# Two probability triangles merged into one square before the transposes, and parted by masks behind them

## The chip, the cores and the metric

The kernel runs on one core of one Trainium2 chip. The metric is the device time of one execution, in microseconds; the comparison uses the median of several runs. A NeuronCore has five engines, each with its own queue of instructions that is worked off in order: TensorE (PE, matrix multiplications and transposes, which write PSUM; PEld is its weight load), VectorE (DVE), ScalarE (ACT), GpSimd (POOL) and SyncE (SP, which issues most DMAs). POOL works on SBUF alone here, and it also issues the gathers.

## The reference

One layer over 4096 tokens of 256 numbers, all in fp32. It adds two branches to the input: a windowed attention block with its feed-forward part, and a mixture of experts (8 experts, the best 2 for each token, 816 hidden units). Both read the normalized input. The change lies in the attention, with 8 heads of 32 numbers:

```python
band = jnp.abs(qi[:, None] - (kj[None, :] - w)) <= w          # w = 64
scores = jnp.einsum('bhcqd,bhckd->bhcqk', q, k3) * scale
scores = jnp.where(allow, scores, jnp.float32(-1e+30))
p = jax.nn.softmax(scores, axis=-1)
o = jnp.einsum('bhcqk,bhckd->bhcqd', p, v3)
...
attn = o @ Wo + bo
x = _layernorm(x + attn, gamma, beta)
h = jax.nn.gelu(x @ W1 + b1, approximate=False)
x = x + (h @ W2 + b2)
```

So a query at position t looks at the keys from t - 64 to t + 64: 129 keys.

## The kernel before

The kernel has four stretches. First come the normalization, the router's logits, the first keys, queries and values, and the table that sorts tokens by expert (to about 82 us). Then a loop of 34 steps, in which each step computes one unit of expert work, a pair of token tiles (256 tokens) or a single one (128). The first 32 steps (`STEPS`) also carry attention. After the loop come five units that may turn out empty (`whole`, from 852 to 888 us), and last the attention branch's feed-forward part with the final sum.

An attention step works on a pair of query tiles i and i + 1 (j is 0 or 1) of 128 queries, and on one half hq of the heads, four heads hh. Even steps have hq = 0, odd steps hq = 1. The queries of a tile look at 256 keys, which start 64 before the tile, so the row of query r has its 129 allowed keys at columns r to r + 128 of these 256. In other words, the first 128 columns hold an upper triangle with its diagonal, the last 128 columns a lower triangle with its diagonal; the rest is zero after the exponential, because the mask has put -1e30 there.

The functions of a step, in the order in which the loop calls them:

- `gather` (L783) issues, on POOL, the indirect DMAs that fetch the tokens of a unit two steps ahead into `xs`, which has three buffers.
- `scores` (L893): 16 half-height matmuls on PE (`ps`, L901) into four PSUM banks; then DVE adds the mask, writes `pr` and keeps the negated maximum (`nm`, L915). `pr` is [128 queries, 4 heads, 2 tiles, 256 keys] and has one buffer.
- `exps` (L927): eight exponentials of 128x256 on ACT (L930), each with its sum; they are called in three portions, with the first two chunks of the expert's up and gate products (`chunk`, L814 on PE, L822 on ACT, L823 on DVE) between them.
- `closing` (L992), in even steps: the output projection of the pair before (L996), the residual's sum and the moments on DVE. `residual` (L985) follows: SP loads a tile and POOL adds the bias (L989).
- `scale` (L939): the reciprocal of the sums, and eight products of 128x256 on DVE (L944), one for each head and tile.
- `down` (L866): the down projection of the unit before (L858, 28 matmuls), its bias on DVE (L871), the store; then the load of the next `wd` on SP.
- `turned` (L796): the transposes of the next unit's tokens (L801) and the copy to `xsT` on DVE (L806). In the steps 1 to 16 a projection for later keys, queries or values follows.
- chunk 2, `flip` for j = 0, chunk 3, `flip` for j = 1. `flip` (L948) transposes, for each half k of the 256 keys, four heads into one PSUM bank (L953), and copies the bank to SBUF as `prT`, on ACT for k = 0 (L960), on DVE for k = 1 (L958).
- chunks 4 and 5, the rest of the hidden units (`glu_rest`, L831), the silu's on ACT (L853).
- `weigh` (L964): 32 matmuls, with 32 columns of `vts` as weights and `prT` as the moving side (L968), into the bank `po`.
- `outputs` (L976), in odd steps only: four activations on ACT (L980) that add `bv` and write `oT`, two for each tile.

The order is written out by hand (`manual_schedule`): each engine runs its instructions in the order of the program's text. All PSUM tiles but `po` share seven banks in rotation (`bank`): a tile gets the bank of the tile seven before it, once that one's reader is through.

Of the kernel before, what the change touches and what calls it, by code (L numbers as in the profile page):

```python
# [41 lines left out]
P = 128  # L42
# [57 lines left out]
def block_kernel(ctx: ExitStack, tc: tile.TileContext, a: dict, out: bass.AP):  # L100
# [23 lines left out]
    def bank(name):  # L124
        return psm.tile([P, G], F32, tag="bank", name=name)

    def halves(pb):
        return pb.rearrange("p (t n) -> p t n", t=2)
# [32 lines left out]
    def bcast(ap, n, at):  # L161

        shape = list(ap.shape)
        shape.insert(at, n)
        return ap.unsqueeze(at).to_broadcast(shape)
# [51 lines left out]
    att = ctx.enter_context(ExitStack())  # L217
    wqkv = pool(att, "wqkv", right)
    mask = wqkv.tile([P, 4, 2 * P], F32, tag="mask", name="mask")
    bqs = wqkv.tile([P, DC], F32, tag="bqs", name="bqs")  # L220
    xnT = wqkv.tile([P, DC, S + 2 * WIN], F32, tag="xnT", name="xnT")
    nc.gpsimd.memset(xnT[:, :, 0:WIN], 0.0)
# [80 lines left out]
    def make_mask():  # L303

        nc.gpsimd.memset(mask, 0.0)
        for kind in range(4):

            def keep(base, step, channel, m=mask[:, kind, :]):  # L310
                nc.gpsimd.affine_select(
                    out=m,
                    in_=m,
                    compare_op=ALU.is_ge,
                    fill=MASKED,
                    base=base,
                    pattern=[[step, 2 * P]],
                    channel_multiplier=channel,
                )

            keep(0, 1, -1)
            keep(2 * WIN, -1, 1)
            if kind == 0:
                keep(-WIN, 1, 0)
            if kind == 3:
                keep(2 * P - WIN - 1, -1, 0)


    with ExitStack() as early:
# [597 lines left out]
    def exps(pr, nm, sums, lo, hi):  # L927
        for n in range(lo, hi):
            hh, j = n // 2, n % 2
            nc.scalar.activation(  # L930
                pr[:, hh, j, :],
                pr[:, hh, j, :],
                AF.Exp,
                bias=nm[:, j, hh : hh + 1],
                scale=-1.0,
                accum_out=sums[:, j, hh : hh + 1],
            )

    def scale(i, hq, pr, sums):  # L939
        rec = sp.tile([P, 2, HQ], F32, tag="rec", name=f"rec{i}_{hq}")  # L940
        nc.vector.reciprocal(rec, sums)
        for j in range(2):
            for hh in range(HQ):
                nc.vector.tensor_scalar(  # L944
                    pr[:, hh, j, :], pr[:, hh, j, :], rec[:, j, hh : hh + 1], None, ALU.mult
                )

    def flip(i, hq, j, pr):  # L948
        prT = []
        for k in range(2):  # L950
            pb = bank(f"pT{i}_{hq}_{j}{k}")
            for hh in range(HQ):
                nc.tensor.transpose(  # L953
                    pb[:, hh * P : (hh + 1) * P], pr[:, hh, j, k * P : (k + 1) * P], ident
                )
            t = sp.tile([P, G], F32, tag="prT", name=f"prT{i}_{hq}_{j}{k}", bufs=4)
            if k:
                nc.vector.tensor_copy(t, pb)  # L958
            else:
                nc.scalar.copy(t, pb)  # L960
            prT.append(t)
        return prT

    def weigh(i, hq, j, prT, po):  # L964
        for k in range(2):
            for hh in range(HQ):
                h = hq * HQ + hh
                nc.tensor.matmul(  # L968
                    po[hh * DH : (hh + 1) * DH, j, hq, :],
                    vts[i + j + k][:, h * DH : (h + 1) * DH],  # L970
                    prT[k][:, hh * P : (hh + 1) * P],
                    start=(k == 0),
                    stop=(k == 1),
                )

    def outputs(i, j, po):  # L976

        oT = sp.tile([P, DC, P], F32, tag="oT", name=f"oT{i + j}")
        for c in range(DC):
            nc.scalar.activation(  # L980
                oT[:, c, :], po[:, j, c, :], AF.Identity, bias=bv[:, c : c + 1]
            )
        return oT

    def residual(i):  # L985

# [2 lines left out]
        nc.gpsimd.tensor_tensor(res, res, bcast(bo, 2, 1), ALU.add)  # L989
        return res  # L990

    def closing(i, oTs, res):  # L992
        pw = halves(bank(f"wo{i}"))
        for j in range(2):
            for c in range(DC):
                nc.tensor.matmul(  # L996
                    pw[:, j, :], oTs[j][:, c, :], Wo[:, c, :], start=(c == 0), stop=(c == DC - 1)
                )
        nc.vector.tensor_tensor(res, pw, res, ALU.add)
        for j in range(2):  # L1000
            moments(mv2[:, i + j, :], res[:, j, :], f"b{i + j}")
        nc.sync.dma_start(out=rows(x1d, i, 2), in_=res)
# [111 lines left out]
    for b in range(ALWAYS):  # L1114

        i, hq = b // 2 * 2, b % 2
        attends = b < STEPS
        hT = hTs[b % 2][:, :, 0 : UNITS[b][1] * P]

        def chunk(f):  # L1120
            glu(b, f, gus[b], xT[b], hT)

        if b + 2 < ALWAYS:
            xs[b + 2] = gather(b + 2)
        if attends:
            pr, nm, sums = scores(i, hq)
        if b == 0:
            xT[0] = turned(0, xs.pop(0))
        if attends:
            exps(pr, nm, sums, 0, 3)  # L1130
        chunk(0)
        if attends:
            exps(pr, nm, sums, 3, 6)
        chunk(1)
        if attends:
            exps(pr, nm, sums, 6, 8)
        if hq == 0 and i - 2 in res:
            closing(i - 2, oTs.pop(i - 2), res.pop(i - 2))
            if i < STEPS:
                res[i] = residual(i)  # L1140
        if attends:
            scale(i, hq, pr, sums)
        if b == STEPS:
            att.close()
            wf = pool(ctx, "wf", right)
            hf = pool(ctx, "hf", right, bufs=2)
            accp = pool(ctx, "accp", right, bufs=4)
            got = pool(ctx, "got", right, bufs=8)
            W1, W2 = matrix(wf, "W1", F1, DC), matrix(wf, "W2", D, FC1)
            b1 = column("b1", FC1, wf)  # L1150
            gamma, beta, b2 = (row(n, D, wf) for n in ("gamma", "beta", "b2"))

            late = pool(ctx, "late", right)
            other.update({n: late for n in range(ALWAYS, BLOCKS, 3)})
            load_unit(ALWAYS)
            for n in range(ALWAYS, BLOCKS):
                xs[n] = gather(n)
        if b == STEPS + 1:
            *_, r2 = rstd_of(mv2, root_of(mv2, NT, "b"), NT, "b")
            x2s[0] = second_loads(0)  # L1160
        if b > 0:
            down(b - 1, downs.pop(b - 1), hTs[(b - 1) % 2])
        if b == ALWAYS - 1:
            load_unit(ALWAYS + 1)
        if b + 1 < ALWAYS:
            downs[b + 1] = load_down(b + 1)
        if b + 1 < ALWAYS:
            xT[b + 1] = turned(b + 1, xs.pop(b + 1))
        else:
            for n in range(ALWAYS, BLOCKS):  # L1170
                xT[n] = turned(n, xs[n])
        g = b // TG
        if attends and g + AHEAD <= NG:
            ahead = g + AHEAD
            if b % TG == 0 and g > 0:
                for c in range(DC):
                    keys(ahead, c)
            elif ahead < NG and b % TG == 1:
                values(ahead * TG + 1, 2, False)
            elif ahead < NG and b % TG == 2:  # L1180
                values(ahead * TG + 3, 2, False)
            elif ahead < NG and b % TG == 3:
                for c in range(DC):
                    queries(ahead, c, False)
        chunk(2)
        if attends:
            if hq == 0:
                pos[i] = pso.tile([P, 2, DC, P], F32, tag="po", name=f"po{i}")
            prT0 = flip(i, hq, 0, pr)
        chunk(3)  # L1190
        silu(hT, 0, 2)
        if attends:
            prT1 = flip(i, hq, 1, pr)
        chunk(4)
        n = b - (ALWAYS - len(MAYBE))
        if n >= 0:
            flags[ALWAYS + n] = nc.values_load(used[0:1, n : n + 1], min_val=0, max_val=1)
        chunk(5)
        silu(hT, 2, 4)
        glu_rest(b, gus[b], xT[b], hT)  # L1200
        silu(hT, 4, FCM)
        silu(hT, FCM, FCE, slice(REM_UP, REM_UP + REM))
        if attends:
            for j, prT in enumerate((prT0, prT1)):
                weigh(i, hq, j, prT, pos[i])
            if hq == 1:
                oTs[i] = [outputs(i, j, pos[i]) for j in range(2)]
        if b + 2 < ALWAYS:
            gus[b + 2] = load_gu(b + 2)

# [124 lines left out]
```

## Time and profile before

| what | value |
|---|---|
| median of 3 runs | 1121.75 us (1121.59 to 1122.61) |
| the profiled execution | 1123.71 us, its span 1121.9 us |
| granted clock of TensorE over the span | 0.999 |
| transposes of `pr` (L953) | 512, 66.8 us busy, 273 ns each |
| exponentials (L930) | 256, 126.7 us busy |
| scaling (L944) | 256, 70.4 us busy, 350 ns each |
| POOL's sum for the residual (L989) | 16, 20.4 us busy |
| gathers of the loop (L788) | 71, 67.7 us busy on POOL |
| length of an odd step without projections | 21.74 us |
| length of an even step without projections | 23.47 us |

The lengths are from start to start of a step's first L901 on the timeline. An engine's busy time says how long it worked, not that the end depended on it. Matmuls overlap, so the time that one costs is to be read from the starts of a row of them. A group's row gives its busy time, the mean length of one, and the idle time that its engine had just before, with what ended it.

### The profile page before, as it was taken

The numbers are of one execution on the slowest core, as the hardware profiler recorded it, in microseconds if no ns is written. First come the engines' busy times: TensorE is split into PE (matmuls) and PEld (weight loads), VectorE is DVE, ScalarE is ACT, GpSimd is POOL, SyncE is SP. The second block draws the span as 40 slices with busy tenths as digits, with TensorE's granted clock in tenths as the row PEclk, the third lists the DMA queues.
The fourth block names the chain that finished last, engine by engine and source line by source line (L and its number), as shares of the span: only waits on it lengthen the run. The fifth ranks groups of instructions, "written<-read, shape, count | busy, mean of one in ns | idle before, by whom it ended". The sixth has DMA issues, their size and how long they took to land. (4 is left out here: it accounts for less than half of the span.)

```text
span 1121.9 us, 18116 instructions
## 1 busy us (share of the span) xinstructions
PE 1108.0 (99%) x6616; PEld 890.2 (79%) x6616; DVE 530.9 (47%) x1635; ACT 533.4 (48%) x1266; POOL 237.9 (21%) x264
## 2 busy tenths in 40 slices
PE   8999999999999999999999999999999999999998
PEld 6578887888888888888888888888888756666667
DVE  6656555455456455554555555545433323333213
ACT  4526456646565556656654666466423421111110
POOL 6421101011010110110101101101203075555422
PEclk9999999999999999999999999999999999999999
DMA  9162444345344443444544544344566423333112
GB/s 288 58 235 76 142 161 160 147 149 181 109 164 171 143 166 135 179 147 154 178 149 149 180 141 175 135 167 146 192 216 234 157 72 99 94 93 94 57 57 75
DMA packets 60746, 163.36 MB, mean 146 GB/s; under 512 B 6288, under 2 KB 46608, under 8 KB 51184
## 3 DMA queue, kind: packets, MB, share of 16 engines
q1 hardware_dynamic: 54176, 144.48, 37.3%
q0 software_dynamic: 6480, 17.70, 5.2%
q8 instruction: 53, 0.87, 0.3%
q14 instruction: 37, 0.30, 0.1%
HBM read 140.28 MB, written 21.89 MB: 145 GB/s over the span
## 5 line engine op out<-in xcount | busy, mean ns | idle before, releaser
L814 PE MATMUL gu<-xsT,wg 128*128 128x256 f32 (+1 forms) x1632 | 357.8, 369 | 1.1 <-ACT xsT L806 0.7
L814 PEld LDWEIGHTS gu<-xsT,wg 128*128 128x128 f32 x1632 | 288.3, 190 | 47.4 <-issue 14.9
L822 ACT ACTIVATE gs<-gu,wg 128x256 f32<-128x256 f32 (+1 forms) x204 | 92.4, 456 | 296.1 <-PE gu L814 269.4
L823 DVE SCALAR_TENSOR_TENSOR hT<-gu,wg,gs 128x256 f32<-128x256 f32 (+1 forms) x204 | 95.1, 468 | 251.6 <-ACT gs L822 243.2
L858 PE MATMUL pe<-wd,hT 128*128 128x256 f32 x896 | 198.9, 379 | 0.0
L858 PEld LDWEIGHTS pe<-wd,hT 128*128 128x128 f32 x896 | 169.9, 190 | 22.9
L989 POOL TENSOR_TENSOR res<-res,bo 128x512 f32<-128x512 f32 x16 | 20.4, 1276 | 597.2 <-DMA res<-xnd 405.7
L930 ACT ACTIVATE pr<-pr,nm 128x256 f32<-128x256 f32 x256 | 126.7, 497 | 0.4
L1052 ACT ACTIVATE hf<-ph,b 128x512 f32<-128x512 f32 x64 | 44.0, 687 | 158.2 <-PE ph L1045 148.9
L1045 PE MATMUL ph<-x2T,W 128*128 128x512 f32 x256 | 111.3, 593 | 0.8 <-DVE x2T L1037 0.8
L1083 PE MATMUL pd<-W,hf 128*128 128x256 f32 x512 | 111.7, 379 | 0.0
L915 DVE CUSTOM_DVE_ANT_0 pr<-ps,mask 128x256 f32<-128x256 f32 x256 | 90.8, 420 | 37.6 <-PE ps L901 37.6
L1083 PEld LDWEIGHTS pd<-W,hf 128*128 128x128 f32 x512 | 96.8, 190 | 13.3 <-issue 0.5
L1045 PEld LDWEIGHTS ph<-x2T,W 128*128 128x128 f32 x256 | 48.5, 190 | 58.9 <-issue 56.9
L788 POOL DMA_INDIRECT xs<-xnd,token x71 | 67.7, 953 | 82.2 <-DVE paired_tiles L755 32.8
L853 ACT ACTIVATE hT<-hT 128x512 f32<-128x512 f32 (+3 forms) x148 | 80.4, 543 | 7.6 <-DVE hT L823 4.2
L1061 POOL DMA_INDIRECT got<-done,slot x64 | 63.3, 989 | 73.9 <-DVE acc L1074 61.0
L944 DVE TENSOR_SCALAR pr<-pr,rec 128x256 f32<-128x256 f32 x256 | 70.4, 350 | 1.1
L953 PE MATMUL pT<-ident,pr 128*128 128x128 f32 x512 | 66.8, 273 | 0.4 <-DVE pr L944 0.3
L953 PEld LDWEIGHTS pT<-ident,pr 128*128 128x128 f32 x512 | 59.7, 141 | 6.7 <-PE gu L814 0.6
L1090 DVE TENSOR_TENSOR acc<-pd,acc 128x512 f32<-128x512 f32 x16 | 11.0, 691 | 83.3 <-PE pd L1083 83.3
L930 ACT ACTIVATION_READ_ACCUMULATOR pr<-pr,nm 128x1 f32 x256 | 48.5, 189 | 0.0
(193 smaller groups left out, 1164.5 us busy)
## 6 DMA issues: line engine op xcount, KB each, us to landing
wg<-in_gate_up SPq DMA_DIRECT2D x37, 1670.5 KB
wd<-in_down SPq DMA_DIRECT2D x37, 1024.0 KB
done<-y SPq DMA_DIRECT2D x30, 256.0 KB
x<-in_x SPq DMA_DIRECT2D x8, 512.0 KB
xnd<-xn SPq DMA_DIRECT2D x8, 512.0 KB
res<-xnd SPq DMA_DIRECT2D x16, 256.0 KB
x1d<-res SPq DMA_DIRECT2D x16, 256.0 KB
x<-x1d SPq DMA_DIRECT2D x8, 512.0 KB
```

What stands on the lines that cost most here:

```text
L788: nc.gpsimd.indirect_dma_start(out=x[:, t, :], out_offset=None, in_=xnd, in_offset=bass.IndirectOffsetOnAxis(ap=token[:, i : i + 1], axis=0),)
L814: nc.tensor.matmul(pb[:, k, :], w[:, lo : lo + P], xT[:, c, :], start=(c == 0), stop=(c == DC - 1),)
L822: nc.scalar.activation(gs, pb[:, 0, :], AF.Identity, bias=w[:, gb : gb + 1])
L823: nc.vector.scalar_tensor_tensor(hT[:, f, :], pb[:, 1, :], w[:, ub : ub + 1], gs, ALU.add, ALU.mult)
L853: nc.scalar.activation(hT[on, lo:hi, :], hT[on, lo:hi, :], AF.Silu)
L858: nc.tensor.matmul(pd[:, t, :], hT[:, f, t * P : (t + 1) * P], w[:, f * D : (f + 1) * D], start=(k == 0), stop=(k == FCE - 1),)
L915: nc.vector.tensor_tensor_reduce(out=pr[:, hh, j, :], in0=ps[hh][:, j, :], in1=mask[:, kind + j, :], scale=-1.0, scalar=-LOWEST, op0=ALU.a ...
L930: nc.scalar.activation(pr[:, hh, j, :], pr[:, hh, j, :], AF.Exp, bias=nm[:, j, hh : hh + 1], scale=-1.0, accum_out=sums[:, j, hh : hh + 1],)
L944: nc.vector.tensor_scalar(pr[:, hh, j, :], pr[:, hh, j, :], rec[:, j, hh : hh + 1], None, ALU.mult)
L953: nc.tensor.transpose(pb[:, hh * P : (hh + 1) * P], pr[:, hh, j, k * P : (k + 1) * P], ident)
L1045: nc.tensor.matmul(ph, W1[:, c, f * P : (f + 1) * P], x2T[:, c, :], start=(c == 0), stop=(c == DC - 1),)
L1083: nc.tensor.matmul(pd[:, u, :], hT[:, f, (t + u) * P : (t + u + 1) * P], W2[:, f, :], start=(f == 0), stop=(f == FC1 - 1),)
```

## The change

The allowed columns of the two halves complement each other: the first half holds keys with column >= row, the second keys with column <= row. They overlap in the diagonal alone. The new kernel adds the second half onto the first, so that a full square is left, and transposes only this square. Behind the transpose two masks of 0 and 1 part it again: `first_keys` keeps keys >= query (with the diagonal), `second_keys` keys < query (without it). What this can't tell apart is the diagonal, where both halves have a value. So the second half's diagonal is kept on its own: the second half is multiplied with the identity, summed along its rows to one number for each query, head and tile (`same`), and multiplied with the difference of the two value rows that belong to it (`xd`, values of the second key tile minus those of the first). This part is transposed too (`pX`, two transposes a step), and is added at the end together with `bv`.

By engines:

- POOL: `merge`, two operations of 128x256 for each head, called between the portions of `exps`; `apart`, two differences of 128x128 a step; the product of `xd` with `same`. At the start, four operations for the two masks.
- DVE: `scale` is one product of 128x1024, one reduction of 128x1024 to 8, and one product of 8. `flip` does two masked evictions for each j, the second one into the freed half of `pr`. `outputs` runs in every step, one addition of 128x256.
- ACT: no copies in `flip`, no `outputs`; one activation a step in `flip_rest`.
- PE: eight transposes in the two calls of `flip` instead of sixteen, and two in `flip_rest`.

```diff
+    first_keys = wqkv.tile([P, P], F32, tag="first_keys", name="first_keys")
+    second_keys = wqkv.tile([P, P], F32, tag="second_keys", name="second_keys")
...
+        for m, base, step in ((first_keys, 0, 1), (second_keys, -1, -1)):
+            nc.gpsimd.memset(m, 1.0)
+            nc.gpsimd.affine_select(
+                out=m,
+                in_=m,
+                compare_op=ALU.is_ge,
+                fill=0.0,
+                base=base,
+                pattern=[[-step, P]],
+                channel_multiplier=step,
+            )
...
-    def scale(i, hq, pr, sums):
+    def merge(pr, hh):
+
+        first, second = pr[:, hh, :, 0:P], pr[:, hh, :, P:]
+        nc.gpsimd.tensor_tensor(first, first, second, ALU.add)
+        nc.gpsimd.tensor_tensor(second, second, bcast(ident, 2, 1), ALU.mult)
+
+    def apart(i, hq):
+
+        xd = sp.tile([P, 2, P], F32, tag="xd", name=f"xd{i}_{hq}", bufs=1)
+        of = slice(hq * P, (hq + 1) * P)
+        for j in range(2):
+            nc.gpsimd.tensor_tensor(
+                xd[:, j, :], vts[i + j + 1][:, of], vts[i + j][:, of], ALU.subtract
+            )
+        return xd
+
+    def scale(i, hq, pr, sums, xd):
+
         rec = sp.tile([P, 2, HQ], F32, tag="rec", name=f"rec{i}_{hq}")
+        same = sp.tile([P, 2, HQ], F32, tag="same", name=f"same{i}_{hq}")
+        by_head = "p j h -> p h j"
         nc.vector.reciprocal(rec, sums)
+        first = pr[:, :, :, 0:P]
+        nc.vector.tensor_tensor(first, first, bcast(rec.rearrange(by_head), P, 3), ALU.mult)
+        nc.vector.tensor_reduce(same.rearrange(by_head), pr[:, :, :, P:], AX.X, ALU.add)
+        nc.vector.tensor_tensor(same, same, rec, ALU.mult)
+        xh = xd.rearrange("p j (h d) -> p j h d", h=HQ)
+        nc.gpsimd.tensor_tensor(xh, xh, bcast(same, DH, 3), ALU.mult)
+
+    def flip(i, hq, j, pr):
+        pb = bank(f"pT{i}_{hq}_{j}")
+        for hh in range(HQ):
+            nc.tensor.transpose(pb[:, hh * P : (hh + 1) * P], pr[:, hh, j, 0:P], ident)
+
+        prT = [sp.tile([P, HQ, P], F32, tag="prT", name=f"prT{i}_{hq}_{j}"), pr[:, :, j, P:]]
+        for t, m in zip(prT, (first_keys, second_keys)):
+            nc.vector.tensor_tensor(
+                t, pb.rearrange("p (h q) -> p h q", h=HQ), bcast(m, HQ, 1), ALU.mult
+            )
+        return prT
+
+    def flip_rest(i, hq, xd):
+
+        pb = halves(bank(f"pX{i}_{hq}"))
         for j in range(2):
-            for hh in range(HQ):
-                nc.vector.tensor_scalar(
-                    pr[:, hh, j, :], pr[:, hh, j, :], rec[:, j, hh : hh + 1], None, ALU.mult
-                )
-
-    def flip(i, hq, j, pr):
...
+            nc.tensor.transpose(pb[:, j, 0:P], xd[:, j, :], ident)
+        added = sp.tile([P, 2, P], F32, tag="added", name=f"added{i}_{hq}", bufs=1)
+        nc.scalar.activation(added, pb[:, :, 0:P], AF.Identity, bias=bv[:, hq : hq + 1])
+        return added
...
-                    prT[k][:, hh * P : (hh + 1) * P],
+                    prT[k][:, hh, :],
...
-    def outputs(i, j, po):
...
+    def outputs(i, hq, po, oT, added):
+        nc.vector.tensor_tensor(oT[:, :, hq, :], po[:, :, hq, :], added, ALU.add)
...
         if attends:
             pr, nm, sums = scores(i, hq)
+            xd = apart(i, hq)
...
             exps(pr, nm, sums, 0, 3)
+            merge(pr, 0)
         chunk(0)
         if attends:
             exps(pr, nm, sums, 3, 6)
+            merge(pr, 1)
+            merge(pr, 2)
         chunk(1)
         if attends:
             exps(pr, nm, sums, 6, 8)
+            merge(pr, 3)
...
-            scale(i, hq, pr, sums)
+            scale(i, hq, pr, sums, xd)
...
+                oTs[i] = sp.tile([P, 2, DC, P], F32, tag="oT", name=f"oT{i}", bufs=1)
             prT0 = flip(i, hq, 0, pr)
         chunk(3)
         silu(hT, 0, 2)
         if attends:
             prT1 = flip(i, hq, 1, pr)
+            added = flip_rest(i, hq, xd)
...
-            if hq == 1:
-                oTs[i] = [outputs(i, j, pos[i]) for j in range(2)]
+            outputs(i, hq, pos[i], oTs[i], added)
```

## The prediction

> **What bounds the kernel now.** I read the page's engine table first, then the window between the routing and the loop's end, then one loop step on each engine.
>
> ```profile
> PE 1108.0 (99%) x6616; PEld 890.2 (79%) x6616; DVE 530.9 (47%) x1635; ACT 533.4 (48%) x1266; POOL 237.9 (21%) x264
> ...
> PEclk9999999999999999999999999999999999999999
> ```
>
> ```profile
> 187.00:805.00 618.00, 618.00 (x4207) 527.18 (x4206) 327.99 (x1054) 363.99 (x908) 66.21 (x66) 1.00 0.45 155
> ```
>
> The columns of the second are the window, its length, busy PE, PEld, DVE, ACT, POOL, the granted clock, the DMA share and GB/s. In the attention steps TensorE has no gap: 618.00 of 618.00 us, at full clock, with DMA at 45%. DVE is busy 53%, ACT 59%, POOL 11%. So here time is PE instructions, and a cut in them is worth its own pace, as long as nothing makes PE wait. "Busy" does not give that pace, since matmuls overlap. I take it from starts on PE's timeline, in step 21 (it starts at 557.02, the first L901; columns are start and length):
>
> ```profile
> 567.69 0.60 PE L801 MATMUL pts<-ident,xs 128*128 128x128 f32 x4
> 568.13 1.89 PE L814 MATMUL gu<-xsT,wg 128*128 128x256 f32 x8
> 569.86 1.04 PE L953 MATMUL pT<-ident,pr 128*128 128x128 f32 x8
> 570.73 1.89 PE L814 MATMUL gu<-xsT,wg 128*128 128x256 f32 x8
> ```
>
> Eight transposes take 570.73 - 569.86 = 0.87 us, or 0.109 us each.
>
> The second thing to read is how long `pr` is finished before PE wants it. The same step on ACT and DVE:
>
> ```profile
> 559.65 0.49 ACT L930 ACTIVATE pr<-pr,nm 128x256 f32<-128x256 f32 x1
> ...
> 563.31 0.50 ACT L930 ACTIVATE pr<-pr,nm 128x256 f32<-128x256 f32 x1
> ```
>
> ```profile
> 563.93 0.20 DVE L941 RECIPROCAL rec<-sums 128x8 f32<-128x8 f32 x1 [0.50 <-ACT pr L930]
> 564.17 2.19 DVE L944 TENSOR_SCALAR pr<-pr,rec 128x256 f32<-128x256 f32 x8
> ```
>
> The exponentials end 6.8 us into the step, the scaling 9.35, the first pT starts at 12.84. That gap of 3.5 us is the cover for all that the change puts between exponentials and transposes. Over all 32 steps pT starts at 12.44 (step 16), 12.84 (the odd steps from 17), 13.77 (3, 7, 11, 15), 14.57 (1, 5, 9, 13 and the even ones from 18), 14.98 (4, 8, 12) and 16.08 (2, 6, 10, 14); in step 0 at 8.55, and there PE already waits for the scaling.
>
> Prices of the pieces:
>
> ```profile
> L989 POOL TENSOR_TENSOR res<-res,bo 128x512 f32<-128x512 f32 x16 | 20.4, 1276 | 597.2 <-DMA res<-xnd 405.7
> ```
>
> ```profile
> L1025 POOL TENSOR_TENSOR x<-x,beta 128x1024 f32<-128x1024 f32 x8 | 18.8, 2348 | 110.8 <-DVE x L1024 110.8
> ...
> L1024 DVE TENSOR_TENSOR x<-x,gamma 128x1024 f32<-128x1024 f32 x8 | 9.8, 1225 | 0.3
> ```
>
> **PE, per step.** Removed: 16 pT. Added: 8 pT and 2 pX. Net 6 fewer, 0.65 us a step, 192 in 32 steps: 192 x 0.109 = 20.9 us. The weighing matmuls stay in number and shape. Two other measures: by busy time (66.8 us over 512, 0.130 each) it is 25.0. The Trainium skill (TensorE: Matmul & The Clock Gate, Part 4) gives about 275 ns for a transpose in a kernel and says that transposes don't keep the clock up; 192 x 0.275 would be 52.8 us. The row agrees with 273 ns as the length of one, but lengths overlap and the granted clock is 1.00, so I take 20.9.
>
> **The Pool chain.** Between exps and scale come eight operations of 128x256, an addition and a multiplication for each head. No row has this shape. The line through 512 (1276) and 1024 (2348) is 0.204 + 2.094 ns per element, which gives 0.74 us at 256 and 0.47 at 128. Each multiplication also waits for the addition before it; L1027, which waits so for L1026, has 0.6 us of idle over 8, 0.075 each. So 0.775 on average. Bounds: half the 512 row, 0.64, and the whole 512 row, 1.28, should two short rows cost like one long one. I take the line, because both its points have row-wise operands with a broadcast too.
> The chain starts when the second exponential is read out, at about 3.3 us (even steps lose their four L980 ahead of exps, 1.14 us on ACT, so they start at the odd steps' time), and is Pool-bound: 3.3 + 8 x 0.775 = 9.5.
> The Trainium skill (GPSIMD Engine Reference, sections 3.1 Elementwise and 4.1 Engine selection) speaks against this: elementwise work belongs on VectorE, GpSimd being about twice as slow; its 4497 ns for 2048 elements makes about 0.56 at 256, an estimate without a fixed part. By it the chain would end at 7.8, by the rows at 9.5; DVE would do the eight at 0.42 (L587, two inputs of 256) in 3.4 us. The ratio is right, but the chain is paid only where it is exposed.
>
> **DVE.** Removed per step: scaling 2.19, two copies L958 at 0.683. Added: one product of 1024 (L1024's 1.225), one reduction of 1024 (L585's 0.42 for 256 and L671's 0.69 for 512 give 1.22), one of 8 (0.19), four masked evictions (0.69 like L871, PSUM with a broadcast operand), one outputs (0.42). That is 5.8 against 3.56: 2.25 more in a step of some 22 us, 63% busy. The new wait stands at the product: behind it on DVE queue y (L871), xsT (L806), the q or v evictions and chunk 2's hT. Product 9.6 to 10.85, so pT may start at 10.9 against 12.44 at the earliest: 1.5 us in hand. Reduction and `same` end at 12.3, y at 13.0 (was 11.55), xsT 13.7, hT 14.2, the first pair of masked evictions 15.6, the second 17.4, before weigh, which comes 0.65 earlier than now, at 20.07. SP's done store and wd load behind y move 1.5 us and have a whole step. PSUM rotates over seven banks: pT1 and pX need those of gu1, wo or pe, which are free by then. In the four short steps (3, 7, 11, 15) two q evictions lie in the same queue and the second masked eviction ends at 18.6 against weigh's second half at 18.45: about 0.15 each, 0.6 us together.
>
> **ACT.** Two L960 (0.576) and on average two L980 (0.368) go, one 128x256 (0.469) comes: 1.4 us less, hidden (59% busy).
>
> **Rest of Pool.** The differences (2 x 0.47) wait for the previous pX and are done before the step starts. The product with `same` waits for DVE at 12.3, ends at 13.2, and pX comes at 15.45: 2.2 in hand. In even steps it stands behind the residual, which waits for its DMA until 11.3 to 13.0: 13.4 to 15.1 against pX at 17.2 (step 16: 14.0 against 15.0). The gathers, which now run two steps ahead, will stand behind this and start 13 to 15 us into a step; they are needed more than a step later. Pool sum: about 7.9 us a step on top of 2 to 4. The four mask operations at the start fall in Pool's idle stretch from 40.3 to 73.1: nothing.
>
> **Step 0** has no down projection, so no cover: additions wait for exps (the last is read at 7.73), the chain ends at 10.1, pT starts at 11.45 instead of 8.55. The old pT0 was itself stretched to 1.5 us by the scaling, so PE is 2.4 late against its gain.
>
> **The sum.** 1123.71 (span 1121.9 and 1.8 around it) - 20.9 + 2.4 + 0.6 = 1105.8 us. The median of the runs, 1121.75, lies 1.96 lower: 1103.8.
>
> At the loop's end PE waits 0.96 us for oT (L980 on ACT), which goes to DVE; up to 2 us may be gained or lost there, left at nothing.
>
> **Rivals.**
> 1. *The Pool chain is exposed (other side).* Place: pT0's wait for the product. It ends at 3.3 + 8p + 1.33, p being Pool's time per operation. Up to p = 0.98 no step but 0 waits; at 1.21 the waits eat the 20.9. At the upper bound (1.276 and its wait, 1.31) it ends at 15.1: eight steps lose 2.26, step 16 loses 2.66, four lose 1.33, eleven 0.53, three 0.12, step 0 about 5.9: 38 us, so +17, 1139. For it: no row of this shape, and Pool's spans are rough. Against: two rows on one line. A smaller exposure, p near 1.1, costs 10 and gives 1111.
> 2. *DVE and Pool hold each other up*, or DVE's queue makes PE wait for a bank or for prT. Against: the product is the one long DVE operation with two SBUF inputs, and Pool idles then. For: 2.25 us more stand in one stretch. One microsecond exposed in each of the 31 steps that have cover gives 1135, half of that 1119.
> 3. *The transposes don't cost what they seem*, because weight loads set the pace and shift to the neighbours: then about 1121. Against: the starts show 0.87 us with nothing else running.
>
> **How the numbers follow.** Forecast 0.66; exposed chain 0.24 (0.19 slower, 0.03 faster, 0.02 no change); DVE 0.07 (0.03, 0.03, 0.01); nothing gained 0.03 (0.02 no change, 0.01 slower). So faster 0.72, same 0.05, slower 0.23, with 0.2% (2.2 us) about what a measurement can tell. The forecast's own range is 1096 (25.0 and 2 at the loop's end, no loss) to 1110. For 8 in 10 it reaches into the exposed cases, 1096 to 1128.
>
> **What would show it.** Right: pT 256 and pX 64 on PE; odd steps from 17 last 21.1 instead of 21.74; L901 to L901 gaps without PE idle; Pool's addition near 0.74; the product starts near 9.6 us into a step. Wrong: idle time of PE before pT ended by DVE pr or POOL pr, Pool operations over 0.98 us, or idle time before po ended by the masked evictions.

## The result, and the profile after

The changed kernel takes 1102.48 us (median, 1102.08 to 1105.73), the kernel before on the same chip 1121.67 us (1121.21 to 1122.61). The ratio is 0.9831, with a 95% interval of 0.9813 to 0.985. The forecast was 1103.8 us.

The profiled execution after took 1102.41 us, its span is 1100.7 us. First the engine table and the row of granted clocks from the page, then the window of the attention steps (its length; busy PE, PEld, DVE, ACT, POOL with their instructions; granted clock, DMA share, GB/s):

```profile
PE 1084.8 (99%) x6424; PEld 868.7 (79%) x6424; DVE 591.3 (54%) x1571; ACT 495.3 (45%) x1170; POOL 502.7 (46%) x620
...
PEclk9999999999999999999999999999999999999999
```

```profile
187.00:785.00 598.00, 598.00 (x4018) 507.81 (x4021) 377.95 (x999) 330.06 (x827) 285.90 (x359) 1.00 0.47 160
```

PE issues 192 instructions fewer. It still has no gap in the steps, although POOL is now busy 48% of that window instead of 11%, and DVE 63% instead of 53%. Step 21 on PE's timeline (start and length; it starts at 545.02), and below it the transposes of step 0:

```profile
556.13 1.89 PE L830 MATMUL gu<-xsT,wg 128*128 128x256 f32 x8
557.86 0.60 PE L987 MATMUL pT<-ident,pr 128*128 128x128 f32 x4
558.30 1.89 PE L830 MATMUL gu<-xsT,wg 128*128 128x256 f32 x8
...
93.59 0.63 PE L987 MATMUL pT<-ident,pr 128*128 128x128 f32 x4 [2.29 <-DVE pr L978]
```

Four transposes take 558.30 - 557.86 = 0.44 us, again 0.11 us each, and they start 12.84 us into the step as before. Only step 0 waits: 2.29 us for the product.

The span, cut at the first score matmul of steps 0 and 1, at the end of the last output product (`po`, step 31) and at the next down projection (`pe`, step 32):

| stretch | before, us | after, us | difference | forecast |
|---|---|---|---|---|
| up to step 0 | 82.75 | 83.00 | +0.25 | 0 |
| step 0 | 18.09 | 18.93 | +0.84 | +1.75 |
| steps 1 to 31 | 704.04 | 683.74 | -20.30 | -19.65 |
| the loop's end | 7.33 | 5.21 | -2.12 | 0 |
| the rest | 309.70 | 309.79 | +0.09 | 0 |
| span | 1121.9 | 1100.7 | -21.2 | -17.9 |

(The forecast's parts are its own terms: 0.65 for each step's transposes, 2.4 for step 0, 0.6 for the short steps.) Each of the steps 1 to 31 is 0.65 us shorter: the even ones from 18 take 22.81 instead of 23.47, the odd ones from 17 take 21.09 instead of 21.74, the short ones 19.10 instead of 19.75. Two lines are off, step 0 and the loop's end. And the profiled executions differ by 21.3 us, the medians by 19.2.

How the new chain ran in step 21, on ACT, POOL and DVE (start, length; in brackets the idle time before and what ended it):

```profile
546.69 1.28 ACT L946 ACT_TABLE_LOAD   x1 [0.86 <-DVE nm L931]
547.99 0.51 ACT L946 ACTIVATE pr<-pr,nm 128x256 f32<-128x256 f32 x1
```

```profile
549.15 0.72 POOL L958 TENSOR_TENSOR pr<-pr 128x256 f32<-128x256 f32 x1 [8.38 <-ACT pr L946]
549.96 0.72 POOL L959 TENSOR_TENSOR pr<-pr,ident 128x256 f32<-128x256 f32 x1
...
553.61 0.72 POOL L958 TENSOR_TENSOR pr<-pr 128x256 f32<-128x256 f32 x1
554.41 1.76 POOL L959 TENSOR_TENSOR pr<-pr,ident 128x256 f32<-128x256 f32 x1
```

```profile
554.37 1.23 DVE L978 TENSOR_TENSOR pr<-pr,rec 128x1024 f32<-128x1024 f32 x1 [1.39 <-POOL pr L958]
556.21 1.22 DVE L979 TENSOR_REDUCE same<-pr 128x8 f32<-128x1024 f32 x1 [0.62 <-POOL pr L959]
```

One thing is to be seen in each. ACT's table load now stands behind a wait and starts 1.67 us into the step; the kernel before (step 21 starting at 557.02) had it without one, at 0.82:

```profile
557.84 1.28 ACT L930 ACT_TABLE_LOAD   x1
```

POOL's operation takes 0.72 us, and the next addition comes 0.7 to 0.8 us later. DVE's product starts as soon as the last *addition* (L958, 553.61 + 0.72) is through; the last multiplication, which runs beside the product, takes 1.76 us instead of 0.72, and the reduction waits 0.62 us for it.

### The profile page after: what moved, and what is told of

It is laid out like the page before. It is cut to its first block, busy times and chain, and to the rows that moved or that the text cites. A ratio compares the mean times of both kernels' runs of the same rounds, so it can differ in the third digit from the quotient of the medians.

```text
span 1100.7 us, 18039 instructions
## 1 busy us (share of the span) xinstructions
PE 1084.8 (99%) x6424; PEld 868.7 (79%) x6424; DVE 591.3 (54%) x1571; ACT 495.3 (45%) x1170; POOL 502.7 (46%) x620
## 5 line engine op out<-in xcount | busy, mean ns | idle before, releaser
L958 POOL TENSOR_TENSOR pr<-pr 128x256 f32<-128x256 f32 x128 | 92.9, 726 | 253.6 <-ACT pr L946 253.6
L959 POOL TENSOR_TENSOR pr<-pr,ident 128x256 f32<-128x256 f32 x128 | 126.2, 986 | 10.0
L1118 PEld LDWEIGHTS pd<-W,hf 128*128 128x128 f32 x512 | 96.9, 190 | 13.3 <-issue 0.5
L1060 POOL TENSOR_TENSOR x<-x,beta 128x1024 f32<-128x1024 f32 x8 | 18.8, 2350 | 94.4 <-DVE x L1059 94.4
L978 DVE TENSOR_TENSOR pr<-pr,rec 128x1024 f32<-128x1024 f32 x32 | 39.2, 1225 | 27.7 <-POOL pr L958 27.7
```

The costliest lines, as they stand in the source:

```text
L958: nc.gpsimd.tensor_tensor(first, first, second, ALU.add)
L959: nc.gpsimd.tensor_tensor(second, second, bcast(ident, 2, 1), ALU.mult)
L1118: nc.tensor.matmul(pd[:, u, :], hT[:, f, (t + u) * P : (t + u + 1) * P], W2[:, f, :], start=(f == 0), stop=(f == FC1 - 1),)
```

## The experiments

The kernel before was run beside each, on the same chip. Its median was 1123.87 us beside the first four, 1123.88 beside the next three, 1121.68 and 1123.44 beside the last ones. Times from different chips are not compared; stretches of the trace are.

### Are the transposes worth 0.109 us each? (e1)

The changed kernel, with each of the eight transposes issued twice:

```diff
         for hh in range(HQ):
-            nc.tensor.transpose(pb[:, hh * P : (hh + 1) * P], pr[:, hh, j, 0:P], ident)
+            for _ in range(2):
+                nc.tensor.transpose(pb[:, hh * P : (hh + 1) * P], pr[:, hh, j, 0:P], ident)
```

> The changed kernel with each of the eight square transposes of a step done twice into the same place (256 more in all, results unchanged). Theory: PE is the bound, a transpose costs its pace of 0.109 us: 256 x 0.109 = 27.9, so 1130.4 us, with no PE gap outside step 0. By busy time (0.130 each) it would be 1135.8. Rival (transposes are hidden by weight loads or by other work): 1102.5.

Median 1132.7 us (1129.51 to 1133.77), ratio 1.0081 (1.0064 to 1.0097). PE's timeline of step 21:

```profile
575.42 1.04 PE L988 MATMUL pT<-ident,pr 128*128 128x128 f32 x8
576.29 1.89 PE L830 MATMUL gu<-xsT,wg 128*128 128x256 f32 x8
```

Eight take 0.87 us, and the step 21.96 us, 0.87 more than with eight fewer. No step but step 0 has a gap. Steps 1 to 31 take 710.81 us together instead of 683.74: 248 more transposes cost 27.07 us, 0.109 each. (The median lies 3 us above the profiled execution, whose clock was 0.999; the others' was 0.996 to 0.997.) So the term of 20.9 us holds in both directions, and the third rival (transposes cost nothing, as others set the pace) falls.

### How much cover was left? (e2)

One more addition on POOL ahead of each merging addition, into a scratch tile:

```diff
+        extra = sp.tile([P, 2, P], F32, tag="extra", name=f"extra{len(extras)}", bufs=1)
+        nc.gpsimd.tensor_tensor(extra, first, second, ALU.add)
         nc.gpsimd.tensor_tensor(first, first, second, ALU.add)
```

> The changed kernel with one more addition of 128x256 on GpSimd ahead of each merge, into a scratch tile that nobody reads: four a step, about 0.80 us each with its wait, 3.2 us. Theory: the chain has cover up to the first transpose. The product then starts at 12.6 us into a step instead of 9.4 and the transposes can begin at 13.95: the odd steps from 17 wait 1.1 us each, step 16 1.5, the four short steps 0.2, steps with transposes at 14.57 or later nothing, step 0 about 3: 14 us, 1117. In the four short steps VectorE's queue is late as well and may cost up to 3.7 each, so up to 1131. Rival A (GpSimd's work is hidden whatever it is): 1102.5. Rival B (each microsecond of the chain counts): 3.2 x 32 = 102, 1205.

Median 1129.24 us (1129.16 to 1130.47), ratio 1.005 (1.0033 to 1.0067). The product now runs from 12.58 to 13.80 us into a step, 3.2 later. PE's timeline, in step 21 and in step 0:

```profile
575.34 1.89 PE L830 MATMUL gu<-xsT,wg 128*128 128x256 f32 x8
578.17 0.68 PE L992 MATMUL pT<-ident,pr 128*128 128x128 f32 x4 [0.94 <-DVE pr L983]
```

```profile
89.08 1.89 PE L830 MATMUL gu<-xsT,wg 128*128 128x256 f32 x8
95.90 1.09 PE L992 MATMUL pT<-ident,pr 128*128 128x128 f32 x4 [4.92 <-DVE pr L983]
96.78 3.62 PE L830 MATMUL gu<-xsT,wg 128*128 128x256 f32 x8
```

Step 21 is 1.20 us longer than in the changed kernel. The eight odd steps from 17 lose 9.6 us together, step 16 loses 1.6, steps whose transposes come at 14.57 or later lose nothing. So far this is the first rival's arithmetic. The four short steps lose 2.61 each, 10.4 together, and not by the first transposes, which come only 0.18 us late. PE's timeline in step 3 (start 153.81):

```profile
167.76 0.63 PE L992 MATMUL pT<-ident,pr 128*128 128x128 f32 x4
168.22 1.06 PE L830 MATMUL gu<-xsT,wg 128*128 128x128 f32 x8
170.34 0.66 PE L992 MATMUL pT<-ident,pr 128*128 128x128 f32 x4 [1.07 <-DVE y L887]
171.03 0.41 PE L1005 MATMUL pX<-ident,xd 128*128 128x128 f32 x2
171.60 2.05 PE L830 MATMUL gu<-xsT,wg 128*128 128x128 f32 x16 [0.16 <-DVE qt L283]
```

The second transposes wait for DVE's `y` (L887), which empties a PSUM bank and stands in DVE's queue behind the late product; the next chunk then waits for the queries' eviction, and the weighing 0.17 us for a masked eviction. Counted in starts against the same step of the changed kernel, the second transposes come 1.43 us late, the next chunk 2.03, the next step 2.61. Step 0 loses 5.1. The sum, 26.7 us, agrees with the spans (1127.5 - 1100.7 = 26.8). So the place and the mechanism of the first rival were real, and in the short steps the second rival's, DVE's queue, joins it. A chain of 3.2 us more eats the whole gain.

Step 0 lost 5.1 us, though its wait grew by 2.6 only (2.29 to 4.92). The windows of that stretch (same columns as above) show the rest:

```profile
93.00:94.00 1.00, 0.00 (x0) 0.00 (x0) 0.00 (x0) 0.00 (x0) 0.92 (x3) 1.00 0.00 0
94.00:95.00 1.00, 0.00 (x0) 0.00 (x0) 0.47 (x1) 0.00 (x0) 0.92 (x2) 0.59 0.00 0
95.00:96.00 1.00, 0.10 (x1) 0.13 (x2) 0.75 (x1) 0.00 (x0) 1.00 (x1) 0.50 0.00 0
...
100.00:101.00 1.00, 1.00 (x5) 0.81 (x4) 0.06 (x1) 0.55 (x2) 0.00 (x0) 0.50 0.51 115
101.00:102.00 1.00, 1.00 (x8) 0.92 (x7) 1.00 (x3) 1.00 (x1) 0.44 (x2) 1.00 0.04 16
```

The granted clock falls to 0.50 at about 94.2 (the 0.59 of that row), some 3.2 us after PE went idle (90.97), and is back at 1.00 only at 101, 5.1 us after PE had work again (95.90). Meanwhile eight `gu` matmuls take 3.62 us instead of 1.89. The Trainium skill (TensorE: Matmul & The Clock Gate, Part 1) says that the clock is halved after an idle window of about 3.4 us and comes back after a busy one, and that these windows run on their own beat, not from the moment at which PE stops or starts. The row agrees: the clock was halved for 6.8 us, as long as two such windows, and in the first of them PE still stood idle until 95.90. In the changed kernel the wait of 2.29 us in step 0 left the clock at 1.00.

### Who moved the table load? (e3)

The two merging operations on VectorE instead of GpSimd:

```diff
-        nc.gpsimd.tensor_tensor(first, first, second, ALU.add)
-        nc.gpsimd.tensor_tensor(second, second, bcast(ident, 2, 1), ALU.mult)
+        nc.vector.tensor_tensor(first, first, second, ALU.add)
+        nc.vector.tensor_tensor(second, second, bcast(ident, 2, 1), ALU.mult)
```

> The changed kernel with the merges (four additions and four multiplications a step) on VectorE instead of GpSimd. Theory (both places are under the cover): 1102.5 less up to 1 for step 0; VectorE 80% busy in the steps; the first exponential back at 2.1 us into a step, from 2.97, because it no longer has to wait for GpSimd as well. Rival (without GpSimd VectorE becomes the bound, masked evictions come late for the weighing): PE gaps before po, 3 us or more slower.

Median 1102.62 us (1101.41 to 1103.39), ratio 0.9806 (0.979 to 0.9823). ACT's timeline of step 21, which starts at 546.35 here:

```profile
547.17 1.28 ACT L946 ACT_TABLE_LOAD   x1
548.47 0.51 ACT L946 ACTIVATE pr<-pr,nm 128x256 f32<-128x256 f32 x1
```

The load is back at 0.82 us, without a wait, and the first exponential at 2.12 instead of 2.97. The operations on ACT are the same in the two kernels; what differs is whether the exponential must wait for POOL as well as for DVE. The trace of the changed kernel has the wait for DVE as an entry of its own ahead of the load, and the exponential behind the load waits for a semaphore that POOL alone raises; the kernel before and this one have no such entry, and their exponential waits for DVE itself. So the second wait moved the first one ahead of the load. VectorE needs 0.42 us for each of the eight, the product comes at 8.1 us in odd steps, and the steps are as long as with GpSimd (21.09, 22.81, 19.10; 683.74 us for steps 1 to 31 in both). So it does not matter here which engine merges, while the work has cover; doing it on VectorE, which the forecast weighed, is worth only 0.5 us, in step 0 (18.44 instead of 18.93).

### Is the slow multiplication the shared port? (e4)

The product as eight instructions with one tile source and one scalar for each row:

```diff
-        nc.vector.tensor_tensor(first, first, bcast(rec.rearrange(by_head), P, 3), ALU.mult)
+        for j in range(2):
+            for hh in range(HQ):
+                nc.vector.tensor_scalar(
+                    first[:, hh, j, :], first[:, hh, j, :], rec[:, j, hh : hh + 1], None, ALU.mult
+                )
```

> The changed kernel with the product of the square and the reciprocals as eight products of 128x128 with a number for each partition, so that VectorE has one tensor from SBUF instead of two while GpSimd does its last multiplication. Theory (the two engines lock each other out where both read two SBUF tensors): the last multiplication is back from 1.76 us to 0.73 and the reduction no longer waits for it; the time stays at 1102.5 because all this is covered. Rival (it is long for another reason, such as writing the tile that VectorE reads): it stays at 1.7.

Median 1101.75 us (1101.3 to 1102.19), ratio 0.9803 (0.9787 to 0.982). The groups of the multiplication and the reduction (shapes, count, busy us, mean ns, idle us before), first of the changed kernel, then of this one:

```profile
L959 POOL TENSOR_TENSOR pr<-pr,ident 128x256 f32<-128x256 f32 x124 | 122.3, 986 | 9.7
...
L979 DVE TENSOR_REDUCE same<-pr 128x8 f32<-128x1024 f32 x31 | 37.9, 1221 | 19.1 <-POOL pr L959 19.1
```

```profile
L959 POOL TENSOR_TENSOR pr<-pr,ident 128x256 f32<-128x256 f32 x124 | 91.3, 736 | 9.7
...
L983 DVE TENSOR_REDUCE same<-pr 128x8 f32<-128x1024 f32 x31 | 37.4, 1207 | 0.0
```

The multiplication's mean falls from 986 ns to 736, the level of the addition, and the reduction's wait of 19.1 us is gone, although POOL and DVE still work beside each other. So the delay came from the form of the product, and not from sharing the tile, which both forms do. The Trainium skill (SBUF — State Buffer, "Who interferes with whom") has a reason: a VectorE instruction with two SBUF inputs and a GpSimd instruction that reads SBUF exclude each other. The numbers agree: 1.76 - 0.72 = 1.04 us of delay against a product of 1.23. The edit does two things at once, though: it takes away the second input and makes eight short instructions of one long one, and no run parts them. The steps are as long as before: the delay was hidden.

### Is step 0 only short of cover? (e7)

In step 0 alone, one chunk of expert matmuls moved ahead of each half of the transposes:

```diff
         chunk(2)
+        if b == 0:
+            chunk(3)
...
-        chunk(3)
+        if b > 0:
+            chunk(3)
+        else:
+            chunk(4)
...
-        chunk(4)
+        if b > 0:
+            chunk(4)
```

> The changed kernel with step 0's order alone changed on PE: chunk 3 ahead of the first transposes, chunk 4 ahead of the second, so that they fill the wait for the product. Theory (the 2.3 us gap of PE in step 0 is the chain without cover): the gap falls under 0.9, 2 us less, 1100.4. Rival (the gap comes back at the second transposes, at pX or at the weighing): under 1 us less.

Median 1101.28 us (1100.29 to 1103.05), ratio 0.9795 (0.9781 to 0.9808). Step 0 takes 17.21 us instead of 18.93, its wait for the product is 0.48 us instead of 2.29, and steps 1 to 31 take 683.74 us as before.

### Where did the 2.1 us at the loop's end come from? (e5, e6, e8, e11, e12)

PE's timeline of the kernel before, from the last `po` of step 31 to the first `pe` of step 32, then that of the changed one:

```profile
803.80 1.08 PE L968 MATMUL po<-prT,vt 128*32 128x128 f32 x32
804.81 1.99 PE L814 MATMUL gu<-xsT,wg 128*128 128x256 f32 x8
806.98 1.13 PE L814 MATMUL gu<-xsT,wg 128*128 128x256 f32 x4 [0.17 <-issue]
808.40 1.02 PE L814 MATMUL gu<-xsT,wg 128*128 128x256 f32 x4 [0.30 <-issue]
810.38 1.99 PE L996 MATMUL wo<-Wo,oT 128*128 128x256 f32 x8 [0.96 <-ACT oT L980]
812.21 5.99 PE L858 MATMUL pe<-wd,hT 128*128 128x256 f32 x27
```

```profile
785.60 3.72 PE L830 MATMUL gu<-xsT,wg 128*128 128x256 f32 x16
789.16 1.89 PE L1031 MATMUL wo<-Wo,oT 128*128 128x256 f32 x8
790.89 6.21 PE L874 MATMUL pe<-wd,hT 128*128 128x256 f32 x28
```

Before, PE stands still three times, twice "issue" (waiting for nothing that the profile shows) and once for `oT` from ACT. ACT had been ready to write it since its last `hT` ended (805.62):

```profile
809.96 1.14 ACT L980 ACTIVATE oT<-po,bv 128x128 f32<-128x128 f32 x4 [4.34 <-PE gu L814]
```

It reads `po`, whose last product ended at 804.88, and yet PE let it go only at 809.96; this is called PE's report below. The forecast saw the 0.96 us and asked what becomes of `oT`. Theory A was that ACT is late there, since the change moves `oT` to DVE. So that move alone, in the kernel before:

```diff
-            nc.scalar.activation(
-                oT[:, c, :], po[:, j, c, :], AF.Identity, bias=bv[:, c : c + 1]
-            )
+            nc.vector.tensor_scalar(
+                oT[:, c, :], po[:, j, c, :], bv[:, c : c + 1], None, ALU.add
+            )
```

> The kernel before with only the outputs moved: the bias bv is added by VectorE instead of ScalarE. It tests the 2.1 us that the changed kernel gains at the loop's end beyond the transposes. Theory A (gained because oT no longer waits for ScalarE): PE's gaps at the loop's end go, 1119.6. Theory B (gained because the late gathers moved out of the way): 1121.7, gaps stay.

Median 1123.67 us (1123.33 to 1126.09), ratio 0.9999 (0.9991 to 1.0007); the loop's end takes 7.32 us with all its gaps. Theory A falls: now DVE waited 4.9 us for the same report. Theory B: the gathers for the last units crowd the end of the loop. They are POOL's next instructions, and in the two kernels they start at different times (before, then after):

```profile
799.82 0.94 POOL L788 DMA_INDIRECT xs<-xnd,token  x1 [25.02 <-DVE hT L823]
```

```profile
794.86 0.99 POOL L804 DMA_INDIRECT xs<-xnd,token  x1 [17.02 <-DMA x1d<-res]
```

Before, the first gather comes 5.1 us *ahead* of the end of `po` (804.88); after the change, it waits, by the profile, for a store of the residual and comes 9.2 us *behind* it (785.67). A first attempt to hold them back put their call one step later:

```diff
-            for n in range(ALWAYS, BLOCKS):
-                xs[n] = gather(n)
         if b == STEPS + 1:
+            for n in range(ALWAYS, BLOCKS):
+                xs[n] = gather(n)
```

> The kernel before with only the gathers of the five late units issued one step later (step 33 instead of 32). Theory B (these gathers and the weights' load crowd out what PE and ScalarE need at the loop's end): the gaps go, 1119.6. Theory A (oT on ScalarE): 1121.7, gaps stay.

Median 1125.22 us (1123.31 to 1126.92), ratio 1.0006 (0.9998 to 1.0014), the loop's end 7.24 us. But POOL has nothing else to do there and issued the gathers at 799.70 all the same: the run says nothing on theory B. So POOL got something to wait for, ahead of the gathers in its queue:

```diff
         nc.vector.tensor_tensor(res, pw, res, ALU.add)
+        if i == STEPS - 2:
+            hold = sp.tile([P, 2], F32, tag="hold", name="hold", bufs=1)
+            nc.gpsimd.tensor_tensor(hold, res[:, 0, 0:2], res[:, 0, 0:2], ALU.add)
```

> The kernel before, with one small GpSimd instruction that reads the residual tile of the last pair of row tiles after its addition on VectorE, ahead of the seven late gathers on GpSimd's queue. So the gathers can start only at about 813 us, after the loop's last outputs, instead of 799.8 us. Theory B (the gathers run beside the last outputs and hold up TensorE's reports at the loop's end): the stretch from the last output product of step 31 to step 32's first one falls from 7.3 us to 5.2 us, the gaps of 0.17, 0.30 and 0.96 us go, and the kernel is about 2 us shorter, a ratio near 0.998, as the gathers themselves are wanted only at 836 us. Theory C (the gathers have nothing to do with it, and the 7.3 us come from how step 32's own work stands): the stretch stays at 7.3 us and the ratio at 1.000.

In its profile the loop's end takes 5.22 us, without a gap. Yet the medians are 1121.45 us (1121.13 to 1123.93) and 1121.68 (1120.98 to 1123.66) for the kernel before, ratio 1.0 (0.9991 to 1.0009). Either the gain was given back, or the kernel before did not have the stall on that chip. The trace is against the first (the rest takes 309.78 us, as before). So the kernel before itself was profiled, and the held one timed beside it, on another chip:

> The kernel before itself, for the loop's end alone. Its median was 1123.9 us on the chips of the first seven experiments and 1121.7 us on that of the last three, while the changed kernel stood near 1102 us on all of them. Theory D (in some executions and not in others, the reports of TensorE are held up beside the late gathers, and the 2.1 us between 7.3 us and 5.2 us at the loop's end are that difference): a median near 1123.9 us goes with 7.3 us at the loop's end in this run's profile, one near 1121.7 us with 5.2 us. Theory E (the chips differ in something else, or the profile itself brings the stall): 7.3 us at the loop's end whatever the median is.

> The kernel before with its late gathers held until the residual of the last pair of row tiles is summed, once more, beside the kernel before on the same chip. The loop's end takes 5.2 us in its profile in either case. Theory D: where the kernel before stands near 1123.9 us this one stands near 1121.7 us, a ratio of 0.998, and where it stands near 1121.7 us both are equal. Theory E: equal in either case, or 2 us shorter in either case.

Here the kernel before took 1124.11 us (1123.34 to 1125.33; 1123.44 in the runs beside it, to which the ratios refer), with 7.36 us at the loop's end in its profile. The held one took 1121.81 us (1121.1 to 1122.72), ratio 0.9981 (0.9972 to 0.999). Its PE timeline:

```profile
804.00 1.08 PE L968 MATMUL po<-prT,vt 128*32 128x128 f32 x32
805.01 3.72 PE L814 MATMUL gu<-xsT,wg 128*128 128x256 f32 x16
808.57 1.89 PE L996 MATMUL wo<-Wo,oT 128*128 128x256 f32 x8
810.30 6.21 PE L858 MATMUL pe<-wd,hT 128*128 128x256 f32 x28
```

One small instruction on POOL takes the three gaps away (5.21 us) and, on this chip, 0.2% off the kernel. So on this chip, where the kernel before stands at 1123.4 us, the early gathers cost it about 2 us; on that of e8, where it stands at 1121.7 us, holding them gains nothing. Theory D holds in so far. Three things stay open: no profile shows the kernel before *without* the stall, none shows by what way the gathers hold up PE's issue and reports, and no run put the gathers early in the *changed* kernel, so that they were the cause there too is carried over from the kernel before.

### The mends together (e9, e10)

The changed kernel with the edits of e4 and e7, and beside it the changed kernel as it is:

> The changed kernel with both mends together: in step 0 chunk 3 stands ahead of the first transposes and chunk 4 ahead of the second, and the product runs as eight instructions of one source and a scalar. If TensorE sets the end in every step but step 0, only step 0 counts: the wait before its first transposes falls from 2.29 us to at most 0.48 us, the span is 1.7 to 2.3 us below the unmended changed kernel of this call, and steps 1 to 31 keep 21.09, 22.81 and 19.10 us. If the lock between VectorE and GpSimd cost the steps anything, they would be shorter than these, up to 1.0 us each; I expect nothing there.

> The changed kernel as it is, on the same chip as the two others: a ratio of 0.981 to 0.985 to the kernel before, step 0 at 18.9 us with 2.3 us of waiting, the loop's end at 5.2 us with the gathers issued only at about 795 us. It is the yardstick for the filled one.

Together 1099.97 us (1099.31 to 1103.27), ratio 0.9808 (0.9793 to 0.9823); as it is 1103.23 us (1101.71 to 1103.39), ratio 0.983 (0.9817 to 0.9844). PE's timeline in step 0 of the mended one, the first transposes and the first of `pX`:

```profile
94.81 0.66 PE L991 MATMUL pT<-ident,pr 128*128 128x128 f32 x4
...
97.96 0.33 PE L1004 MATMUL pX<-ident,xd 128*128 128x128 f32 x1 [0.32 <-POOL xd L986]
```

No idle time is left before the transposes, and 0.32 us before `pX`. Step 0 takes 16.97 us instead of 18.93; steps 1 to 31 take 683.74 us in both. The traces so give 2.0 us; the medians differ by 3.3, the lowest times by 2.4. The expected span, 1.7 to 2.3 us below, did not show in the profiled executions (1100.3 against 1100.0): the mended one reached step 0 at 84.96 us, the other at 82.48. This is the fastest version found.

## Why the forecast was right, and where not

The main term and its mechanism were right. That the total came within 1.3 us is in part luck: the span fell by 3.3 us more than forecast, and a step to the median of 2.0 us did not come.

- **The transposes, -20.9 us: right.** 31 steps gave 20.3, step 0's share is within its own line, and e1 measured the same price by adding.
- **POOL's chain: right at the end, by two errors that offset each other.** The operation was taken at 0.74 us and measured 0.726; the chain was to end at 9.5 and the product to start at 9.6, and in the step shown it started at 9.35. But the chain starts at 4.13 us, not at 3.3, because the exponentials' new wait for POOL pushed the table load 0.85 us back (e3). And the product does not wait for the whole chain, as the forecast had it, but for the last addition only, which saves the last multiplication, 0.7 to 0.8 us.
- **The short steps, +0.6 us: did not come.** The forecast had the second masked eviction end at 18.6 us there, against 18.45 for the matmuls that need it; it ended at 18.09.
- **Step 0, +2.4 us: right in kind, too large.** The loss against the transposes' own gain was 0.84 + 0.65 = 1.49 us. The transposes start at 10.58 us, not at 11.45: there too the product waits for the last addition alone. That cover is what is missing, e7 shows.
- **The loop's end, nothing: wrong in the profiled execution.** The forecast read the 0.96 us as a wait for ACT and allowed for up to 2 us either way, without a reason. It was part of a stall of 2.1 us that goes when the gathers come later (e8 and e12, in the kernel before), and the change delays them by accident: by the profile they now wait for a store. The forecast followed the gathers inside a step, but not at the loop's end.
- **The step from the profiled execution to the median, -1.96 us**, was taken for the same in both kernels. It was not: before, the profiled execution lay 2.0 us above the median, after, at the median. This fits the stall, which the profiled execution had and the runs timed for the median seem not to have had; no trace of theirs shows it. So the two omissions offset each other in part, which nobody planned: 17.9 us were forecast, 21.3 came between the profiled executions, 19.2 between the medians.
- **The first rival** (an exposed chain) did not happen, but e2 shows that its mechanism is real: 3.2 us more of chain and the kernel is slower than before.
- **The second rival** did not happen either, but was argued away by a false statement: that POOL idles during the product. It runs the last multiplication then, and is held up by 1.04 us in each step, and DVE's reduction by 0.62. This costs nothing (e4: the steps keep their lengths), since what waits for the reduction has slack: in step 21 the product of `xd` with `same` ended at 13.3 us and was wanted at 15.45.

## What to carry to other kernels

Where one engine has no gap, price a cut in its work by the distance between starts (0.109 us), not by an instruction's length (0.273 us), and spend the rest of the thought on the cover: how late may the new chain end in each kind of step, and which step has none. When a step is lengthened on one engine, look for what stands behind it in the *other* queues too: in e2 four short steps lost 10.4 us by what stood behind the product on DVE, eight odd ones 9.6 us by the wait itself. An instruction that gets a second engine to wait for may pull its first wait ahead of something that used to run free (0.85 us of table load here), and a transfer that starts earlier than it need may cost more than a late one (about 2 us at the loop's end).

## What the hardware showed beside that

- A long wait of PE can cost more than its length. 2.29 us of idling in step 0 left the granted clock at 1.00; 4.92 us halved it for some 6.8 us and cost another 2.4. Where between the two the limit lies was not measured.
- Executions differ by 1.3 to 3.1 us ahead of the loop: step 0 starts at 82.3 to 83.0 us in nine profiles and at 84.3 to 85.4 in five, of the kernel before (82.75 and 84.33) as of the changed one. In all five late ones (e3, e5, e7, e9, e11) the clock granted from 10 to 15 us was 0.84 to 0.92 and from 15 to 20 us 0.74 to 0.82; in the nine others it was 1.00. A median of few runs carries this, so for effects of this size the stretches of the trace decide.
- Beside the seven early gathers PE was held up by 2.1 us at the loop's end, in instructions that touch none of their data. By the times with the gathers held back (ratio 0.9981 in e12, 1.0 in e8) this seems not to happen on every chip.
